# Gated cross-attention with a mixture of experts: values of four heads in quarters of the matmul array, scores in row halves, K and V without zero padding

## The chip, the cores and the metric

The kernel runs on one core of one Trainium2 chip, in float32. The metric is the device time in microseconds (us) of one execution; lower is better. Engines are named as in the profile: PE (TensorE, matmuls) and PEld (its weight loads), DVE (VectorE), ACT (ScalarE), POOL (GpSimd), SP (SyncE, here an issuer of transfers). Matmuls write to PSUM, from where DVE or ACT read.

## The reference

Four sequences of 1024 tokens with 256 features attend to 64 context rows each with 16 heads of 64; the result is multiplied by the query, projected, gated and added. A mixture of 8 experts (two of them per token) follows. Cut to what matters:

```python
# x (4, 1024, 256), ctx_1024 (4, 64, 256), 16 heads of 64
qh = einsum('bld,hdk->hblk', layernorm(x), w_qs)
kh = einsum('bld,hdk->hblk', ctx, w_ks)
vh = einsum('bld,hdk->hblk', ctx, w_vs)
attn = softmax(einsum('hblk,hbmk->hblm', qh, kh), axis=-1)
out = einsum('hblm,hbmk->hblk', attn, vh) * qh
x = x + tanh(g_xattn) * (out.reshape_heads() @ w_proj.T + b_proj)
# experts: 8, F = 1024, top 2 by gate logits, softmax over the two
h = silu(einsum('td,edf->tef', layernorm(x), w1))
x = x + tanh(g_ffn) * (einsum('tef,efd->ted', h, w2) combined by the two weights)
```

## The kernel before

**Tiling.** The 4096 tokens go in 8 groups g of 512 (two groups to a sequence, so sequence b = g // 2), a group in 4 tiles t of 128. The 16 heads go in 8 pairs p; a pair's two heads of 64 fill the 128 partitions. `NP` is 8, `DK` and `M` (head size, context rows) are both 64, `P` is 128.

**K and V.** One block `kv[b]` for each of the four sequences (L168) holds both, for each pair as a 128 x 128 block-diagonal matrix: head j has rows and columns of half j, and the other two quarters stay zero from a memset on POOL (L170). `keys` (L284) computes K of two pairs into one PSUM bank and copies it out in eight 64 x 128 pieces (L302; on DVE for the first two pairs, on ACT for the rest). `values` (L306) copies V with four 64 x 256 pieces on ACT for each bank (L323).

**Queries, scores, softmax.** `queries` (L337) makes qT, the queries of a group transposed (128 partitions of a pair, 512 tokens), in two matmuls for a pair (L341), and ACT copies them out of PSUM. `probabilities` (L352) makes the scores of a tile with 8 matmuls, one for a pair, with qT of the tile as weights and the pair's 128 x 128 K block as the streamed operand (L355). DVE takes the maximum (L364) and subtracts it (L366), ACT takes the exponential (L369), DVE sums (L371) and inverts, POOL multiplies (L374). `transpose_probabilities` (L379) transposes a pair at a time on PE (L384), and ACT copies to aT (L385).

**Values.** `attend` (L390) makes for each pair one matmul, V's block as weights and aT of the group's 512 tokens as the streamed operand (L393), into a PSUM bank of its own, and DVE multiplies the result with qT in place (L394). `project` (L396) follows with L402 and adds to the residual stream.

**Order.** The loop at L996 runs over groups and tiles: scores of this tile, transposes of the tile before it, queries of the next group (L1009), then `finish` (L944) for the group before: at t = 1 all of `attend`, at t = 2 and 3 `project`. The tile framework turns the written order into one instruction list for each engine with its own planning, so neighbouring pieces can be interleaved. Calls marked `keep_in_program_order` stay where they are written. From group 6 on pieces of the experts' work (`run_slots`) are woven in. POOL's list entries and token gathers are issued behind the newest softmax multiply (`behind_softmax`, L750).

**Buffers.** PSUM has two pools: `ps2`, two tiles of two banks each, takes the scores; `ps1`, four single banks, takes everything else (`bank`, L100), among it queries, transposes, values and projections. In SBUF blocks of one "share" take turns in a number of equal buffers: "weight" has seven (wq, wp, the four kv, and the expert weights as they come).

Of the kernel before, what the change touches and what calls it, by code (L numbers as in the profile page):

```python
# [8 lines left out]
F32 = mybir.dt.float32  # L9
I32 = mybir.dt.int32  # L10
AF = mybir.ActivationFunctionType
ALU = mybir.AluOpType
# [3 lines left out]
P = 128  # L16
# [5 lines left out]
def kernel(  # L22
# [13 lines left out]
    w2: bass.AP,  # L36
    out: bass.AP,
):

# [16 lines left out]
    nc = tc.nc  # L58

    B, L, D = x.shape  # L60
    M = context.shape[1]
    H, _, DK = w_qs.shape
    E, _, F = w1.shape
# [4 lines left out]
    GB = L // G  # L68
    NP = H // 2
# [20 lines left out]
    rows = ctx.enter_context(tc.tile_pool(name="rows", bufs=2))  # L90
# [3 lines left out]
    ps2 = ctx.enter_context(tc.tile_pool(name="ps2", bufs=2, space=PSUM))  # L94
    ps1 = ctx.enter_context(tc.tile_pool(name="ps1", bufs=4, space=PSUM))

    def block(shape, name, share):
        return blocks.tile(shape, F32, tag=share, bufs=shares[share], name=name)

    def bank(name, spare=False):  # L100

        if spare:
            return ps2.tile([P, 2, 512], F32, tag="ps2", name=name)[:, 0]
        return ps1.tile([P, 512], F32, tag="ps1", name=name)
# [60 lines left out]

    kv = [block([P, 2, NP, P], f"kv{b}", "weight") for b in range(B)]  # L168
    for t in kv:
        nc.gpsimd.memset(t, 0.0)  # L170

    ident = const.tile([P, P], F32, tag="ident", name="ident")
    make_identity(nc, ident)
# [110 lines left out]
    def keys(ctxT):  # L284
        for p0 in range(0, NP, 2):
            pk = bank(f"pk_{p0}").rearrange("p (i n) -> p i n", i=2)
            for i in range(2):
                for c in range(NC):
                    nc.tensor.matmul(
                        pk[:, i, :],  # L290
                        wk[:, c, (p0 + i) * P : (p0 + i + 1) * P],
                        ctxT[:, c, :],
                        start=(c == 0),
                        stop=(c == NC - 1),
                    )
            pkv = pk.rearrange("p i (b m) -> p b i m", m=M)
            for j in range(2):
                rows = slice(j * DK, (j + 1) * DK)
                copy = nc.scalar.copy if p0 else nc.vector.tensor_copy
                for b in range(B):  # L300
                    tc.keep_in_program_order(
                        copy(kv[b][rows, 0, p0 : p0 + 2, j * M : (j + 1) * M], pkv[rows, b])  # L302
                    )
            yield

    def values(ctxT):  # L306

        n = 512 // P
        for b0 in range(0, B, 2):
            for p0 in range(0, NP, n):  # L310
                pv = bank(f"pv_{b0}_{p0}")
                for c in range(NC):
                    nc.tensor.matmul(
                        pv,
                        ctxT[:, c, b0 * M : (b0 + 2) * M],
                        wv[:, c, p0 * P : (p0 + n) * P],
                        start=(c == 0),
                        stop=(c == NC - 1),
                    )
                pvv = pv.rearrange("p (i j k) -> p i j k", j=2, k=DK)  # L320
                for i in range(2):
                    for j in range(2):
                        nc.scalar.copy(  # L323
                            kv[b0 + i][j * M : (j + 1) * M, 1, p0 : p0 + n, j * DK : (j + 1) * DK],
                            pvv[i * M : (i + 1) * M, :, j, :],
                        )
                yield

# [5 lines left out]
    def of_pair(t, p):  # L334
        return t[p // (NP // 2)][:, p % (NP // 2), :]
# [14 lines left out]
    newest = []  # L350

    def probabilities(g, t, qT):  # L352
        sc = ps2.tile([P, NP, 2 * M], F32, tag="ps2", name=f"sc_{g}_{t}")
        for p in range(NP):
            nc.tensor.matmul(  # L355
                sc[:, p, :],
                of_pair(qT, p)[:, t * P : (t + 1) * P],
                kv[g // GB][:, 0, p, :],
                start=True,
                stop=True,  # L360
            )
        scv = sc.rearrange("p i (j m) -> p (i j) m", m=M)
        mx = small.tile([P, H], F32, tag="mx", name=f"mx_{g}_{t}")
        nc.vector.tensor_reduce(mx, scv, AX.X, ALU.max)  # L364
        pr = soft.tile([P, H, M], F32, tag="pr", name=f"pr_{g}_{t}")
        nc.vector.tensor_tensor(  # L366
            pr, scv, mx.unsqueeze(2).to_broadcast([P, H, M]), ALU.subtract
        )
        nc.scalar.activation(pr, pr, AF.Exp)  # L369
        sm = small.tile([P, H], F32, tag="sm", name=f"sm_{g}_{t}")  # L370
        nc.vector.tensor_reduce(sm, pr, AX.X, ALU.add)  # L371
        nc.vector.reciprocal(sm, sm)  # L372
        newest[:] = [
            nc.gpsimd.tensor_tensor(pr, pr, sm.unsqueeze(2).to_broadcast([P, H, M]), ALU.mult).ins  # L374
        ]
        return pr

    def transpose_probabilities(g, t, pr, aT):
        prv = pr.rearrange("p (i j) m -> p i (j m)", j=2)  # L379
        n = 512 // P  # L380
        for p0 in range(0, NP, n):
            pt = bank(f"pa_{g}_{t}_{p0}")
            for i in range(n):
                nc.tensor.transpose(pt[:, i * P : (i + 1) * P], prv[:, p0 + i, :], ident)  # L384
            nc.scalar.copy(  # L385
                aT[p0 // n][:, :, t * P : (t + 1) * P], pt.rearrange("p (i q) -> p i q", i=n)
            )

    def attend(g, pairs, qT, aT):

        for p in pairs:
            po = bank(f"po_{g}_{p}")
            nc.tensor.matmul(po, kv[g // GB][:, 1, p, :], of_pair(aT, p), start=True, stop=True)  # L393
            nc.vector.tensor_tensor(of_pair(qT, p), po, of_pair(qT, p), ALU.mult)  # L394

    def project(g, qT, t0):  # L396

        pp = bank(f"pp_{g}_{t0}").rearrange("p (t d) -> p t d", d=D)
        for i in range(2):
            t = t0 + i  # L400
            for p in range(NP):
                nc.tensor.matmul(  # L402
                    pp[:, i, :],
                    of_pair(qT, p)[:, t * P : (t + 1) * P],
                    wp[:, p, :],
                    start=(p == 0),
                    stop=(p == NP - 1),
                )
        nc.vector.scalar_tensor_tensor(
            xg[g][:, t0 : t0 + 2, :], pp, tg[:, 0:1], xg[g][:, t0 : t0 + 2, :], ALU.mult, ALU.add  # L410
        )
# [265 lines left out]
    half = len(tiles) // 2  # L677
# [264 lines left out]
    held = {}  # L942

    def finish(g, step):  # L944

        qT, aT = held[g]
        if step == 1:
            attend(g, range(NP), qT, aT)
        elif step >= 2:
            project(g, qT, (step - 2) * 2)  # L950

# [44 lines left out]
    for g in range(NG + 1):  # L996
        attention_ends = g == NG
        if g < NG:
            qT, aT = q_next, halves(f"aT_{g}")
            held[g] = (qT, aT)  # L1000
        if g + 1 < NG:
            q_next = halves(f"qT_{g + 1}", "hidden" if g % 3 == 1 else "group")
        for t in range(T):
            if g < NG:
                pr = probabilities(g, t, qT)
            if last:
                transpose_probabilities(*last)
            if g + 1 < NG:
                queries(g + 1, q_next, parts[g > 0][t])  # L1009
            if 0 <= g - 1 < NG:  # L1010
                finish(g - 1, t)
            last = (g, t, pr, aT) if g < NG else None

            if g >= GB + 1:
                b = (g - GB - 1) // GB
                after(b * GB + GB - 1, (g - GB - 1) % GB * T + t)
            if g == 0 and t == 1:
                tc.keep_in_program_order(nc.scalar.activation(tg, tg, AF.Tanh))
                tc.keep_in_program_order(
                    nc.gpsimd.tensor_scalar(bias, bias, tg[:, 0:1], None, ALU.mult)  # L1020
                )
                for h in range(2):
                    add_bias(h)
            if g + 2 < NG:
                if t == 0 and (g + 2) % GB == 0:
                    stats = ln_stats(list(range(g + 2, g + 2 + GB)), f"a{g + 2}")
                elif t == 2:
                    ln_norm(g + 2, stats, "a")
                    add_bias(g + 2)
            if g == 0:  # L1030
                next(pending_values)
            for _ in range(pieces[g][t] if g in pieces else 0):
                next(slots)
# [5 lines left out]
    for _ in slots:  # L1039
# [3 lines left out]
    _, used = nc.values_load_multi_w_load_instructions(  # L1043
        in_use[0:1, 0:1], min_val=0, max_val=NB, bass_reorder=False
    )
# [38 lines left out]
```

## Time and profile before

| | |
|---|---|
| Runs shown | 945.53, 956.56, 959.87 us; median 956.56 |
| Profiled execution | 945.0 us, of which the span is 943.3 |
| Mean granted PE clock | 0.985 |
| L355, scores on PE | 512 instructions, mean 276 ns |
| L393, values on PE | 128 instructions, mean 593 ns |
| L341, queries on PE | 256 instructions, mean 596 ns |
| L402, projection on PE | 512 instructions, mean 379 ns |
| L384, transposes of probabilities on PE | 256 instructions, mean 278 ns |
| L394, multiplies on DVE | 64 instructions, median 680 ns |

All durations come from one profiled execution. The durations of matmuls overlap, since the next one starts while the last one still passes through the array, so their sum is not the time that they take; the distance from one start to the next is. Weight loads run beside the matmul before them. Busy time of other engines costs nothing as long as PE doesn't wait for them.

### The profile page before, as it was taken

The numbers are of one execution on the slowest core, as the hardware profiler recorded it, in microseconds if no ns is written. First come the engines' busy times: TensorE is split into PE (matmuls) and PEld (weight loads), VectorE is DVE, ScalarE is ACT, GpSimd is POOL, SyncE is SP. The second block draws the span as 40 slices with busy tenths as digits, with TensorE's granted clock in tenths as the row PEclk, the third lists the DMA queues.
The fourth block names the chain that finished last, engine by engine and source line by source line (L and its number), as shares of the span: only waits on it lengthen the run. The fifth ranks groups of instructions, "written<-read, shape, count | busy, mean of one in ns | idle before, by whom it ended". The sixth has DMA issues, their size and how long they took to land. (4 is left out here: it accounts for less than half of the span.)

```text
span 943.3 us, 11358 instructions
## 1 busy us (share of the span) xinstructions
PE 904.0 (96%) x4176; PEld 703.8 (75%) x4176; DVE 327.3 (35%) x733; ACT 254.7 (27%) x390; POOL 409.8 (43%) x395
## 2 busy tenths in 40 slices
PE   6989999999999996899998999999999999999995
PEld 4555858586768766587897887777777888888884
DVE  7364485647755876444138000000000000000010
ACT  3464242433342323342123121122121121121110
POOL 3051212113532254325636656755544554555343
PEclk9999999999999999899998999999999999999998
DMA  9500000100010002724773465745444455657110
GB/s 211 175 1 0 1 23 1 45 23 24 1 45 23 23 1 88 247 68 118 183 236 108 117 224 191 256 133 165 168 168 149 142 162 196 230 165 269 59 45 30
DMA packets 87789, 106.50 MB, mean 113 GB/s; under 512 B 29348, under 2 KB 73770, under 8 KB 87728
## 3 DMA queue, kind: packets, MB, share of 16 engines
q1 hardware_dynamic: 62784, 70.50, 24.4%
q0 software_dynamic: 11840, 25.25, 8.5%
q10 hardware_dynamic: 13104, 9.96, 3.6%
q8 instruction: 35, 0.57, 0.3%
q14 instruction: 26, 0.21, 0.1%
HBM read 89.60 MB, written 17.65 MB: 114 GB/s over the span
## 5 line engine op out<-in xcount | busy, mean ns | idle before, releaser
L809 PE MATMUL ph<-xT,w 128*128 128x256 f32 (+1 forms) x960 | 242.6, 410 | 0.7 <-ACT xT L782 0.7
L865 PE MATMUL py<-w,hT 128*128 128x256 f32 x1088 | 242.6, 382 | 0.0
L865 PEld LDWEIGHTS py<-w,hT 128*128 128x128 f32 x1088 | 206.4, 192 | 27.6
L809 PEld LDWEIGHTS ph<-xT,w 128*128 128x128 f32 x960 | 182.7, 191 | 52.1 <-ACT xT L782 1.1
L817 ACT ACTIVATE hT<-ph 128x1024 f32<-128x1024 f32 (+2 forms) x80 | 71.6, 896 | 390.2 <-PE ph L809 383.7
L848 DVE TENSOR_SCALAR x<-py,ids 128x256 f32<-128x256 f32 x68 | 32.9, 483 | 403.9 <-PE py L865 370.0
L374 POOL TENSOR_TENSOR pr<-pr,sm 128x1024 f32<-128x1024 f32 x32 | 61.4, 1919 | 228.8 <-DVE sm L372 218.3
L341 PE MATMUL pq<-nT_a,wq 128*128 128x512 f32 x256 | 115.9, 596 | 0.6 <-ACT nT_a L260 0.6
L402 PE MATMUL pp<-wp,qT 128*128 128x256 f32 x512 | 113.1, 379 | 0.0
L402 PEld LDWEIGHTS pp<-wp,qT 128*128 128x128 f32 x512 | 97.1, 190 | 18.2 <-issue 5.5
L831 POOL DMA_INDIRECT x<-out_dram,ids x68 | 69.9, 1028 | 88.4 <-DMA out_dram<-x,ids 62.0
L758 POOL DMA_INDIRECT x<-normed,ids x68 | 68.2, 1003 | 45.5 <-DMA ids<-lists 26.4
L850 POOL TENSOR_TENSOR x<-x,x 128x256 f32<-128x256 f32 x68 | 49.3, 725 | 82.6 <-DVE x L848 78.6
L341 PEld LDWEIGHTS pq<-nT_a,wq 128*128 128x128 f32 x256 | 46.6, 192 | 47.7 <-issue 45.4
L508 POOL DMA_INDIRECT lists<-entry,to_row x64 | 62.4, 975 | 42.9 <-DVE entry L498 19.5
L851 POOL DMA_INDIRECT out_dram<-x,ids x68 | 69.7, 1024 | 19.2 <-POOL x L850 17.7
L355 PEld LDWEIGHTS sc<-kv,qT 128*128 128x128 f32 x512 | 62.0, 192 | 7.6 <-issue 6.2
L355 PE MATMUL sc<-kv,qT 128*128 128x128 f32 x512 | 64.4, 276 | 0.7 <-DVE pr L366 0.6
L385 ACT COPY aT<-pa 128x512 f32<-128x512 f32 x64 | 34.5, 589 | 96.0 <-PE pa L384 86.5
L393 PE MATMUL po<-aT,kv 128*128 128x512 f32 x128 | 56.5, 593 | 0.1
L364 DVE TENSOR_REDUCE mx<-sc 128x16 f32<-128x1024 f32 x32 | 38.9, 1219 | 37.3 <-PE sc L355 37.1
L371 DVE TENSOR_REDUCE sm<-pr 128x16 f32<-128x1024 f32 x32 | 38.8, 1217 | 21.9 <-ACT pr L369 21.9
(180 smaller groups left out, 652.2 us busy)
## 6 DMA issues: line engine op xcount, KB each, us to landing
w<-in_L_ffn_w_dram SPq DMA_DIRECT2D x60, 1024.0 KB, 7.6
out_dram<-x ACTq DMA_DIRECT2D x8, 512.0 KB, 3.7
normed<-keep_b ACTq DMA_DIRECT2D x8, 512.0 KB, 2.9
x<-in_x_dram SPq DMA_DIRECT2D x7, 512.0 KB, 7.5
x<-normed,ids POOLq DMA_INDIRECT x68, 5.9
x<-out_dram,ids POOLq DMA_INDIRECT x68, 4.9
out_dram<-x,ids POOLq DMA_INDIRECT x68, 2.5
wv<-in_L_xattn_w_vs_dram SPq DMA_DIRECT2D x2, 512.0 KB, 7.1
```

The costliest lines, as they stand in the source:

```text
L341: nc.tensor.matmul(pq, wq[:, c, p * P : (p + 1) * P], nT[g][:, c, :], start=(c == 0), stop=(c == NC - 1),)
L355: nc.tensor.matmul(sc[:, p, :], of_pair(qT, p)[:, t * P : (t + 1) * P], kv[g // GB][:, 0, p, :], start=True, stop=True,)
L374: nc.gpsimd.tensor_tensor(pr, pr, sm.unsqueeze(2).to_broadcast([P, H, M]), ALU.mult).ins
L393: nc.tensor.matmul(po, kv[g // GB][:, 1, p, :], of_pair(aT, p), start=True, stop=True)
L402: nc.tensor.matmul(pp[:, i, :], of_pair(qT, p)[:, t * P : (t + 1) * P], wp[:, p, :], start=(p == 0), stop=(p == NP - 1),)
L508: nc.gpsimd.indirect_dma_start(out=lists, out_offset=bass.IndirectOffsetOnAxis(ap=to_row[:, k, i : i + 1], axis=0), in_=entry[:, k, i, :], ...
L758: gather = nc.gpsimd.indirect_dma_start(out=place, out_offset=None, in_=normed[: tokens_of(s)], in_offset=bass.IndirectOffsetOnAxis(ap=ids ...
L809: nc.tensor.matmul(ph[:, i, :], a[:, c, f * P : (f + 1) * P], xT[:, c, :], start=(c == 0), stop=(c == NC - 1),)
L817: nc.scalar.activation(hT[f0 // per_tile][:, f1 : f1 + step, :], ph, AF.Silu)
L831: gather = nc.gpsimd.indirect_dma_start(out=acc[t], out_offset=None, in_=outf[:n], in_offset=bass.IndirectOffsetOnAxis(ap=ids[:, t, 0:1], ...
L851: scatter = nc.gpsimd.indirect_dma_start(out=outf[:n], out_offset=bass.IndirectOffsetOnAxis(ap=ids[:, t, 0:1], axis=0), in_=acc[t], in_off ...
L865: nc.tensor.matmul(py[t], hT[f // per_tile][:, f % per_tile, t * P : (t + 1) * P], b[:, f, :], start=(f == 0), stop=(f == NF - 1),)
```

## The change

K and V lose their padding. One tile `kT` holds K of all sequences, a pair's two heads on the two halves of the partitions; one tile `vs` holds V with the context rows of one head on partitions 0 to 63 and those of another on 64 to 127.

- The memsets go. K of two pairs is copied with one instruction for a bank, by turns on DVE and ACT.
- Scores: for each pair two matmuls in place of one, each with 64 rows (one head's half of the partitions) of qT as weights and 64 columns of K streamed. The two heads of a pair write to different banks of the score tile, which so holds the first heads of all pairs and then the second heads.
- Transposes then pair head r of pair 2q with head r of pair 2q + 1.
- Values: for two pairs (four heads) four matmuls with 64 rows and 64 columns of weights, each in a quarter of the array: rows by j (which of the two pairs), columns by r (which head of the pair). They write to two banks, each half by half. DVE's multiplies stay as they are.
- `attend` now runs in two halves: the first four pairs at t = 1 ahead of the next group's queries, the other four where it was.

```diff
-    kv = [block([P, 2, NP, P], f"kv{b}", "weight") for b in range(B)]
-    for t in kv:
-        nc.gpsimd.memset(t, 0.0)
+    kT = block([P, NP, B, M], "kT", "weight")
+    vs = block([P, B, NP, DK], "vs", "weight")
...
-            pkv = pk.rearrange("p i (b m) -> p b i m", m=M)
-            for j in range(2):
-                rows = slice(j * DK, (j + 1) * DK)
-                copy = nc.scalar.copy if p0 else nc.vector.tensor_copy
-                for b in range(B):
-                    tc.keep_in_program_order(
-                        copy(kv[b][rows, 0, p0 : p0 + 2, j * M : (j + 1) * M], pkv[rows, b])
-                    )
+            copy = nc.vector.tensor_copy if p0 % 4 == 0 else nc.scalar.copy
+
+            tc.keep_in_program_order(
+                copy(kT[:, p0 : p0 + 2].rearrange("p i b m -> p i (b m)"), pk)
+            )
...
-                pvv = pv.rearrange("p (i j k) -> p i j k", j=2, k=DK)
+                pvv = pv.rearrange("p (q j r k) -> p q j r k", j=2, r=2, k=DK)
+                q0 = p0 // 2
                 for i in range(2):
+                    to = vs[:, b0 + i].rearrange("p (r q) k -> p q r k", r=2)
                     for j in range(2):
                         nc.scalar.copy(
-                            kv[b0 + i][j * M : (j + 1) * M, 1, p0 : p0 + n, j * DK : (j + 1) * DK],
-                            pvv[i * M : (i + 1) * M, :, j, :],
+                            to[j * M : (j + 1) * M, q0 : q0 + n // 2],
+                            pvv[i * M : (i + 1) * M, :, j],
                         )
...
-        sc = ps2.tile([P, NP, 2 * M], F32, tag="ps2", name=f"sc_{g}_{t}")
+        sc = ps2.tile([P, 2, NP, M], F32, tag="ps2", name=f"sc_{g}_{t}")
         for p in range(NP):
-            nc.tensor.matmul(
-                sc[:, p, :],
-                of_pair(qT, p)[:, t * P : (t + 1) * P],
-                kv[g // GB][:, 0, p, :],
-                start=True,
-                stop=True,
-            )
-        scv = sc.rearrange("p i (j m) -> p (i j) m", m=M)
+            for r in range(2):
+                of_head = slice(r * DK, (r + 1) * DK)
+                nc.tensor.matmul(
+                    sc[:, r, p, :],
+                    of_pair(qT, p)[of_head, t * P : (t + 1) * P],
+                    kT[of_head, p, g // GB, :],
+                    start=True,
+                    stop=True,
+                )
+        scv = sc.rearrange("p r i m -> p (r i) m")
...
-        for p in pairs:
-            po = bank(f"po_{g}_{p}")
-            nc.tensor.matmul(po, kv[g // GB][:, 1, p, :], of_pair(aT, p), start=True, stop=True)
-            nc.vector.tensor_tensor(of_pair(qT, p), po, of_pair(qT, p), ALU.mult)
+        for q in range(pairs[0] // 2, pairs[-1] // 2 + 1):
+            po = [bank(f"po_{g}_{2 * q + j}") for j in range(2)]
+            for r in range(2):
+                for j in range(2):
+                    half = slice(j * M, (j + 1) * M)
+                    i = r * (NP // 2) + q
+                    nc.tensor.matmul(
+                        po[j][r * DK : (r + 1) * DK],
+                        vs[half, g // GB, i, :],
+                        of_pair(aT, i)[half],
+                        start=True,
+                        stop=True,
+                    )
+            for j in range(2):
+                own = of_pair(qT, 2 * q + j)
+                nc.vector.tensor_tensor(own, po[j], own, ALU.mult)
...
-            attend(g, range(NP), qT, aT)
+            attend(g, range(NP // 2, NP), qT, aT)
...
+            if g and t == 1:
+                attend(g - 1, range(NP // 2), *held[g - 1])
             if g + 1 < NG:
                 queries(g + 1, q_next, parts[g > 0][t])
```

## The prediction

> **What bounds the kernel now.** I read the busy times first, then the table by stage, then who waits for whom in the attention stage, then the order of the matmuls in time.
>
> The page's first part gives busy us, share and count of each engine; below it is the table by stage (stage bounds, length, then busy us of PE, weight loads, DVE, ACT, POOL, granted clock, DMA share, GB/s):
>
> ```profile
> PE 904.0 (96%) x4176; PEld 703.8 (75%) x4176; DVE 327.3 (35%) x733; ACT 254.7 (27%) x390; POOL 409.8 (43%) x395
> ```
>
> ```profile
> 20.00:370.00 350.00, 344.45 (x1650) 243.45 (x1650) 218.62 (x434) 134.10 (x220) 104.83 (x69) 1.00 0.11 30
> 370.00:382.00 12.00, 1.38 (x4) 0.69 (x4) 5.48 (x8) 0.59 (x2) 6.02 (x5) 0.70 0.83 273
> 382.00:480.00 98.00, 96.84 (x457) 79.55 (x458) 35.30 (x87) 28.38 (x39) 45.51 (x45) 0.98 0.52 145
> 480.00:885.00 405.00, 402.09 (x1803) 330.09 (x1802) 50.44 (x159) 77.67 (x103) 221.56 (x235) 0.99 0.55 178
> ```
>
> Attention fills PE from 20 to 370 us (344.45 of 350), the experts fill it from 382 to 885. DVE is at 218.62 of 350 there: not the bound. Between them lies a hole of about 10 us, in which PE waits for the first gathered tokens. The waits of PE from 60 to 360 us are one line long:
>
> ```profile
> PE pa L384 <- POOL pr L374: 0.6, 1, 0.6
> ```
>
> So the price of an edit is what it does to the time PE needs to pass its instructions. Durations do not show that, as matmuls overlap; the distance from start to start does. The timeline of PE (start, us to the end of the piece, instruction, count):
>
> ```profile
> 129.50 1.95 PE L355 MATMUL sc<-kv,qT 128*128 128x128 f32 x16
> 131.29 1.04 PE L384 MATMUL pa<-ident,pr 128*128 128x128 f32 x8
> 132.16 1.88 PE L341 MATMUL pq<-nT_a,wq 128*128 128x512 f32 x4
> 133.88 7.03 PE L393 MATMUL po<-aT,kv 128*128 128x512 f32 x16
> 140.75 1.95 PE L355 MATMUL sc<-kv,qT 128*128 128x128 f32 x16
> ...
> 395.85 1.62 PE L423 MATMUL pl<-gw,nT_b 128*128 128x8 f32 x14
> ```
>
> One tile of scores takes 131.29 - 129.50 = 1.79 us for 16 instructions: 112 ns each. One group's values take 140.75 - 133.88 = 6.87 us for 16: 429 ns each. The program writes 8 matmuls in each case; the trace has 16, so each f32 matmul is two adjacent instructions, each with its own weight load. Over the run that is 512 x 0.112 = 57.3 us of scores and 128 x 0.429 = 54.9 us of values. The last line is the clue for weight loads: 14 logits matmuls stream only 8 columns but still take (1.62 - 0.25)/13 = 105 ns or a little more each (their mean duration 0.25 us). A load of 128 columns therefore passes no faster than about 105 to 112 ns, and the scores stand at that limit already.
>
> [...]
>
> **The change, part by part.** The profiled execution took 945.0 us: span 943.3 and 1.7 around it. The runs shown have a median of 956.56 and go from 945.53 to 959.87, so the profiled one lies at their lower edge. I sum against 945.0.
>
> *Values.* Eight full matmuls of a group become 16 quarter matmuls (64 rows x 64 columns), still 512 columns streamed and two instructions each: 32 instructions. If four quarters run side by side, a group takes 32/4 x 429 ns = 3.43 us instead of 6.87. Eight groups: -27.4 us. [...]
>
> *Scores.* Eight full matmuls with 128 columns streamed become 16 with 64 rows and 64 columns streamed. Streaming halves, but the weights are still 128 columns of qT, and there are 32 loads in a tile instead of 16. If the two row halves load side by side it is 16 load times, 1.79 us as before: 0. If loads pass one at a time it is 32 x 112 = 3.58 us, +1.79 us in each of 32 tiles, +57.3 us. A gain is excluded, because the load pitch binds already. I take 0 and keep +57.3.
>
> *Mode switches.* New: full, half and quarter modes alternate. Two switches for each of 32 score tiles, and two for each of 16 half attends: 64 + 32 = 96, if nothing is interleaved. The trace has none. Lower bound 0[...]. Upper: a matmul's tail, duration less pitch (593 - 429 = 164 ns), plus an exposed load (190 ns): 0.354 us, 34 us in all. I take one exposed load at its pitch, 0.112: +10.8 us.
>
> *Attend in two halves, with pairs of banks.* The multiplies of DVE stay 64 x 0.68 us. Before, eight of them (5.4 us) lay under 6.87 us of PE. Now the first half attend puts four outputs into the four single banks in 0.86 us, right behind a score tile. DVE is then still in that tile's maximum and subtraction (1.22 each, 2.44 from the end of the scores), so the first bank is free at 2.44 + 0.68 = 3.12, while PE wants it for the queries at 0.87 (transposes) + 0.86 = 1.73. Behind that wait are the queries, the second half attend, and through ACT's qT copies the next group. Up to 1.4 us for each of 8 groups, 11 us; 0 if the compiled order has the queries first. I take 6.
>
> *K and V without padding.* Four memsets (7.04 us) leave POOL: 0, since they ended at 9.84 us and the first K copy began at 12.31, released by PE. Thirty-two K copies (8 on DVE, 0.285; 24 on ACT, 0.263) become four of 512 elements, about 0.6 to 0.7 by the ACT and DVE copies of that size at L260. DVE begins the first statistics at 14.15 right after its eight copies; one wide copy ends 1.1 us earlier, but the transposes also wait for the last key matmul at 17.8, so about 0.5 of the 1.1 arrives: -0.5 us. The 16 V copies keep number and size. Four blocks of the "weight" share become two; they free nothing for the expert weights at 371 us, since kv0 to kv2 were released by then: before, wp and kv3 are held, after, wp and vs, five free either way: 0. No DMA is added or moved; the queues of SP and POOL keep their order, their list entries following the softmax as before.
>
> Sum: 945.0 - 27.4 + 0 + 10.8 + 6 - 0.5 = 933.9 us. Savings before about 357 us pass the hole at 370, because the list entries and gathers that end it follow the softmax, which follows PE. Since two of three runs lie 1.2 and 1.5% above the profiled one, I lean up by 2: 936.
>
> **The rivals.**
>
> *Case 1*, all quarters and halves truly side by side: the sum above; its ends are 945.0 - 27.9 = 917 (switches and bank waits free) and 917 + 34 + 11 = 962.
>
> *Case 2*, the two instructions of one f32 matmul block each other. They are adjacent, on one tile, and start in order: the second waits for the first's stream, and the next tile waits behind it. Then only the second half of one overlaps with the first half of the next: one 429 ns step for each of 16 quarter matmuls, 6.87 us, no gain. With switches, and no bank wait as PE is slow again: 945.0 + 10.8 - 0.5 = 955. For it: the adjacency in the trace. [...]
>
> *Case 3*, the other side: weight loads of the two row halves pass one at a time. Place: L355's loads. 945.0 - 27.4 + 57.3 + 10.8 - 0.5 = 985; it decides as soon as more than half of the doubled loads are not overlapped (28 us). For it: scores stand at the load pitch now, and the number of 128-column loads doubles. [...]
>
> *Case 4*, the change does not do what it says: tiles take turns altogether, +54.9 on values and +57.3 on scores: about 1068.
>
> **Numbers.** Case 1: 0.58; case 2: 0.14; case 3: 0.24; case 4: 0.04. A measurement here cannot tell about 2% from no change, 19 us. Case 1 is faster by that only if switches and waits together stay under 9 us: 0.38 faster, 0.20 within. Case 2: 0.10 within, 0.04 slower (dear switches). Cases 3 and 4 slower. Together 0.38, 0.30, 0.32. Case 1 alone: 917 to 962. The range: 915 at the bottom, below which nothing is worked out, to 992, which takes in case 3 at its price and leaves out its dear half and case 4, some 0.16.
>
> **What would show it.** Values: PE from the first to the last po instruction of a group, 3.4 us (case 1) or 6.9 (case 2). Scores: 32 instructions of a tile in 1.8 us or 3.6. Switches: a gap of 0.1 to 0.35 us between the last tiled and the first full matmul. Bank waits: PE's query matmuls or loads waiting on DVE's L394 successor. I would be wrong if scores fell clearly below 1.79 us a tile (loads cheaper with 64 rows), or if the hole at 370 grew by what attention gained.

## The result and the profile after

The changed kernel is slower: a median of 968.31 us over 20 runs (958.36 to 974.74) beside 955.11 for the kernel before, a ratio of 1.0136 with a 95% interval of 1.0107 to 1.0164. That is under the 2% named in the prediction, but the interval lies wholly above 1. The profiled execution took 959.5 us, with a span of 957.7. The runs of both kernels scatter more here than later, when the kernel before had medians of about 946, but the lowest run of each gives the same ratio (958.36 / 945.52 = 1.0136), and every ratio below is against the runs of before made beside it.

The first part of the page of the changed kernel (busy us, share, count), and of the groups by shape the two that were edited:

```profile
PE 910.3 (95%) x4816; PEld 700.0 (73%) x4816; DVE 319.1 (33%) x727; ACT 253.0 (26%) x368; POOL 404.1 (42%) x391
```

```profile
L358 PE MATMUL sc<-kT,qT 64*128 64x64 f32 x1024 | 72.6, 287 | 0.9 <-issue 0.8
L402 PE MATMUL po<-aT,vs 64*64 64x512 f32 x256 | 37.7, 611 | 1.3 <-issue 1.3
```

Both edits do on PE what was intended: 1024 half and 256 quarter instructions. Their timeline in the stretch that the prediction showed:

```profile
129.22 2.00 PE L358 MATMUL sc<-kT,qT 64*128 64x64 f32 x32
131.15 1.09 PE L387 MATMUL pa<-ident,pr 128*128 128x128 f32 x8
132.17 1.95 PE L402 MATMUL po<-aT,vs 64*64 64x512 f32 x16
134.47 1.98 PE L341 MATMUL pq<-nT_a,wq 128*128 128x512 f32 x4 [0.35 <-DVE qT L411]
136.39 2.09 PE L402 MATMUL po<-aT,vs 64*64 64x512 f32 x16
138.41 2.00 PE L358 MATMUL sc<-kT,qT 64*128 64x64 f32 x32
140.34 1.09 PE L387 MATMUL pa<-ident,pr 128*128 128x128 f32 x8
```

Half an attend has 16 instructions in 1.95 us. They start in fours, 7 ns apart within a four, and the fours start 0.48, 0.43 and 0.43 us apart (from 132.17 us); full instructions that stream 512 columns, that is, pass them through the loaded weights, start 0.43 us apart as well. So four run at a time. A score tile takes 131.15 - 129.22 = 1.93 us with its 32 loads, against 1.79 before. The weight loads (PEld) show why: the thirty-two start in pairs, 7 ns apart, and pass in 1.86 us, two in the time in which one of full height passed before (0.11 us); eight of the quarters pass in 0.21, and a single one lasts 0.13. So the loads of different tiles overlap (a bracket is the idle time before the group).

```profile
129.22 1.86 PEld L358 LDWEIGHTS sc<-kT,qT 64*128 64x128 f32 x32 [0.76 <-issue]
132.17 0.21 PEld L402 LDWEIGHTS po<-aT,vs 64*64 64x64 f32 x8 [0.17 <-issue]
```

From one score tile to the next the stretch shown lasts 138.41 - 129.22 = 9.19 us, against 11.25 before. Little of that is left over a whole group of four tiles: 45.55 us, from the start of a score tile at 83.67 to the same tile of the next group at 129.22, against 45.98 before (83.52 to 129.50). So there is a small gain here; the loss is elsewhere, and the table by stage has it in one column, the granted clock (after the busy times of PE, loads, DVE, ACT and POOL). Before, then after:

```profile
70.00:180.00 110.00, 110.00 (x511) 76.51 (x510) 62.91 (x105) 41.19 (x65) 21.84 (x11) 1.00 0.05 15
180.00:330.00 150.00, 149.35 (x754) 109.62 (x753) 100.13 (x225) 51.70 (x82) 47.94 (x33) 1.00 0.08 22
```

```profile
70.00:180.00 110.00, 108.94 (x715) 73.05 (x714) 63.41 (x106) 42.27 (x66) 21.83 (x11) 1.00 0.05 15
180.00:330.00 150.00, 146.91 (x919) 106.60 (x919) 94.01 (x207) 47.37 (x75) 44.34 (x30) 0.94 0.08 22
```

From 180 to 330 us PE is busy for 146.91 of 150 us, yet its clock fell to 0.94. The clock records of both traces give full or half clock (1.0 or 0.5) and nothing between, and in each trace every record but the last lasts a whole number of times 3.413 us: in the attention stage of the changed kernel four stretches at half, from about 190, 207, 292 and 313 us, of 3.4, 3.4, 6.8 and 3.4 us, where the kernel before has none. Around the hole it stays at half for 23.9 us instead of 10.2. The first of them closely, in stretches of 3.4 us, and the instructions in it:

```profile
186.60:190.00 3.40, 3.40 (x38) 3.24 (x38) 0.59 (x4) 0.00 (x0) 0.00 (x0) 1.00 0.00 0
190.00:193.40 3.40, 3.40 (x11) 2.36 (x12) 2.43 (x2) 2.00 (x3) 0.00 (x0) 0.50 0.47 159
```

```profile
186.59 0.66 PE L358 MATMUL sc<-kT,qT 64*128 64x64 f32 x8
187.18 1.73 PE L440 MATMUL pl<-gw,nT_b 128*128 128x8 f32 x14
188.84 1.10 PE L358 MATMUL sc<-kT,qT 64*128 64x64 f32 x14
189.88 1.89 PE L387 MATMUL pa<-ident,pr 128*128 128x128 f32 x8
```

The table calls PE busy for all 3.40 us of 186.6 to 190.0, and then its clock is halved. At the pitch of 512 columns in 429 ns a column takes 0.84 ns. The 22 half matmuls run in pairs: 11 x 64 x 0.84 = 0.59 us of streaming; the 14 logits add 14 x 8 x 0.84 = 0.09, and the transpose that begins there 0.1. By this estimate PE streamed for about 0.8 of those 3.4 us, while PEld was busy for 3.24 of them. After it eight transposes take 1.89 us instead of 1.09.

### The profile page after: what moved, and what is told of

It reads as the page before. It is cut to its first block, busy times and chain, and to the rows that moved or that the text cites. A ratio compares the mean times of both kernels' runs of the same rounds, so it can differ in the third digit from the quotient of the medians.

```text
span 957.7 us, 12598 instructions
## 1 busy us (share of the span) xinstructions
PE 910.3 (95%) x4816; PEld 700.0 (73%) x4816; DVE 319.1 (33%) x727; ACT 253.0 (26%) x368; POOL 404.1 (42%) x391
## 5 line engine op out<-in xcount | busy, mean ns | idle before, releaser
L341 PE MATMUL pq<-nT_a,wq 128*128 128x512 f32 x256 | 119.7, 611 | 5.0 <-DVE qT L411 4.2
L358 PEld LDWEIGHTS sc<-kT,qT 64*128 64x128 f32 x1024 | 66.4, 197 | 17.6 <-issue 17.3
L358 PE MATMUL sc<-kT,qT 64*128 64x64 f32 x1024 | 72.6, 287 | 0.9 <-issue 0.8
L348 ACT COPY qT<-pq 128x512 f32<-128x512 f32 x64 | 36.6, 582 | 42.6 <-PE pq L341 42.6
```

Of the source, the lines that this page charges most:

```text
L341: nc.tensor.matmul(pq, wq[:, c, p * P : (p + 1) * P], nT[g][:, c, :], start=(c == 0), stop=(c == NC - 1),)
L358: nc.tensor.matmul(sc[:, r, p, :], of_pair(qT, p)[of_head, t * P : (t + 1) * P], kT[of_head, p, g // GB, :], start=True, stop=True,)
```

## The experiments

**The two halves of the change, and three rivals.** The first theory was that the scores in row halves bring the half clock, because they halve the streaming under unchanged loads. Rivals: the quarters bring it; the tiled mode itself does; or mode switches and bank waits eat the gain and the clock is by the way.

The first kernel has the values' part alone, with K padded again in blocks `kb`:

```diff
...
-                    sc[:, r, p, :],
-                    of_pair(qT, p)[of_head, t * P : (t + 1) * P],
-                    kT[of_head, p, g // GB, :],
...
+                sc[:, p // 2, :, p % 2, :],
+                of_pair(qT, p)[:, t * P : (t + 1) * P],
+                kb[g // GB // 2][:, g // GB % 2, p, :],
...
```

> Values in quarters and the attend in two halves as in the change; scores as before: full 128-row matmuls against zero-padded K (the pair's two outputs are written two heads apart so that the transposes keep the change's pairing). Clock theory (it is the scores in row halves, streaming 64 columns under loads of 128, that let the granted clock fall to half): no half-clock window between 75 and 360 us, mean clock 0.985 or better, values 3.4 to 4.5 us of PE a group, and 0.975 to 0.985 of the time before. Rival, values in quarters let the clock fall: half-clock windows stay between 180 and 360 us, mean clock 0.975 or less, ratio 0.99 or more. Rival, switches and bank waits alone eat the gain: clock 0.985 and ratio 0.99 to 1.00.

Measured: ratio 0.9904 (0.9889 to 0.9919). The table by stage and the waits of PE from 60 to 365 us:

```profile
180.00:330.00 150.00, 145.47 (x807) 105.18 (x804) 101.80 (x238) 51.69 (x82) 49.67 (x35) 1.00 0.08 22
```

```profile
PE pq L349 <- DVE qT L417: 4.2, 6, 1.3
PE pa L393 <- POOL pr L383: 1.0, 1, 1.0
PE po L408 <- DVE qT L417: 0.9, 2, 0.7
```

The clock stays at 1.00: the quarters are acquitted. The gain was smaller than I expected from the clock theory and lies in the band of the last alternative, that switches and bank waits eat it. A group's values take 5.0 us (six groups, from the starts of PE's instructions), not 3.4 to 4.5; the waits for the multiplies, 5.1 us in all, are a part of that, as the bank waits of the prediction had it.

The second has the scores' part alone; padded V and whole attend as before, and DVE's subtraction puts the heads back in pairs:

```diff
...
-            pr, scv, mx.unsqueeze(2).to_broadcast([P, H, M]), ALU.subtract
+            pr.rearrange("p (i r) m -> p r i m", r=2),
+            sc,
+            mx.rearrange("p (r i) -> p r i", r=2).unsqueeze(3).to_broadcast([P, 2, NP, M]),
+            ALU.subtract,
...
```

> Scores in row halves with compact K; values as before in full matmuls with padded V, attend in one piece (DVE's subtraction puts the heads back in pairs). Clock theory: half-clock windows between 180 and 360 us as in the change, mean clock 0.975 or less, scores about 0.3 to 0.4 us a tile dearer with their switches (10 to 13 us) plus about 10 us of half clock: ratio 1.015 to 1.03. Rival, the quarters let the clock fall: mean clock 0.985, ratio 1.005 to 1.015. Rival, scores in halves cost nothing: ratio 1.00.

Measured: ratio 1.0172 (1.0154 to 1.0190), mean clock 0.974, and from 180 to 330 us a clock of 0.95, all as the clock theory had it:

```profile
180.00:330.00 150.00, 149.51 (x874) 108.39 (x871) 92.03 (x185) 47.79 (x75) 44.36 (x30) 0.95 0.06 19
```

The loss sits in the scores.

The third keeps the halves but lets each stream 128 columns, so that loads, switches and tiling stay and only the streaming changes:

```diff
+                first = (p * B + g // GB) * M
+                wide = min(2, NP - p) * M
...
-                    sc[:, r, p, :],
+                    sc[:, r].rearrange("p i m -> p (i m)")[:, p * M : p * M + wide],
...
-                    kT[of_head, p, g // GB, :],
+                    kT.rearrange("p i b m -> p (i b m)")[of_head, first : first + wide],
```

> The changed kernel, but each score matmul streams 128 columns of K instead of 64 (the second 64 are the next columns in memory; the next pair overwrites them, and the last pair streams 64): same loads, same row halves, same number of instructions and switches, only the streaming doubles, beneath loads of the same length. Clock theory: a score tile takes no longer than in the change (about 1.9 us) and the half-clock windows between 180 and 360 us go: mean clock about 0.985, ratio 1.000 to 1.006. Rival, it is the tiled mode or its gaps that count as idle: windows stay, ratio 1.013 or more. Rival, the streaming of the two halves doesn't fit beneath the loads: a tile takes 2.5 us or more, ratio above 1.02.

Measured: ratio 1.0030 (1.0004 to 1.0055). A tile of 32 still takes 138.72 - 136.78 = 1.94 us, though each instruction streams twice as much:

```profile
136.78 2.00 PE L360 MATMUL sc<-kT,qT 64*128 64x128 f32 x32
138.72 1.09 PE L389 MATMUL pa<-ident,pr 128*128 128x128 f32 x8
```

The stretches at half clock that lay where logits and scores meet went; two others, of 3.4 us each, came at about 233 and 336 us, each after a window in which PE had waited for a bank (its queries wait 6.2 us for the multiplies in all, 2.5 the longest). More work for PE, and less time (1.0030 against 1.0136): no theory of switches or waits alone gives that.

The fourth puts the whole attend back in one place (`attend(g, range(NP), ...)` in `finish`).

> The changed kernel with all of the attend in one piece at its old place. If bank waits behind the early half attend are what eats the gain: the queries' waits for DVE (4.2 us in all) go and the ratio falls to 1.008 or less. Clock theory: eight outputs in four banks keep PE to the multiplies of DVE, 5.4 us a group against 3.4, so waits grow by about 1 us a group and half-clock windows stay: ratio 1.013 to 1.025.

Measured: ratio 1.0110 (1.0091 to 1.0130), a little under the change and under the band I gave. The waits of PE change their place, from the queries (4.2 us) to the values, also 4.2 us from 60 to 365 us, and the clock stays low (0.95 from 190 to 350 us, as in the change). The split brings nothing to the change, and costs nothing that this run can show.

**Tiling mode or streaming.** The fifth kernel is the one before, with each score matmul cut in two of 64 columns on all 128 rows. Nothing in it is tiled:

```diff
-            nc.tensor.matmul(
-                sc[:, p, :],
-                of_pair(qT, p)[:, t * P : (t + 1) * P],
-                kv[g // GB][:, 0, p, :],
+            for j in range(2):
+                nc.tensor.matmul(
+                    sc[:, p, j * M : (j + 1) * M],
+                    of_pair(qT, p)[:, t * P : (t + 1) * P],
+                    kv[g // GB][:, 0, p, j * M : (j + 1) * M],
...
```

> The kernel before with each score matmul cut in two that stream 64 columns each, on all 128 rows (the padded K, one half of its columns each): no tiling mode anywhere, twice the loads, one after the other. If the share of streaming under the loads is what the clock follows: a tile takes 32 x 112 ns = 3.6 us at full clock, in which PE streams about half of the time, and half-clock windows appear all through the attention stage (mean clock 0.95 or less), ratio 1.075 to 1.13. If the tiling mode is what counts as idle: mean clock 0.985 as before and only the loads' 57 us, ratio 1.055 to 1.065.

Measured: ratio 1.0507 (1.0487 to 1.0526), which misses both bands. A tile takes 103.38 - 99.86 = 3.52 us, so full-height loads do pass one after the other, 0.11 us each:

```profile
99.86 3.68 PE L356 MATMUL sc<-kv,qT 128*128 128x64 f32 x32
103.38 1.04 PE L385 MATMUL pa<-ident,pr 128*128 128x128 f32 x8
```

But the clock is neither low throughout nor as before:

```profile
70.00:180.00 110.00, 110.00 (x575) 81.53 (x573) 55.75 (x91) 33.05 (x53) 21.95 (x12) 1.00 0.02 6
180.00:330.00 150.00, 150.00 (x788) 113.44 (x787) 83.61 (x172) 47.33 (x72) 39.87 (x28) 0.95 0.09 25
```

It falls without any tiling, from 1.00 in the stage without gate logits to 0.95 in the one that has them. Scores alone, which by estimate stream half of the time (64 x 0.84 = 54 ns of each 110), don't bring it; scores and logits together do. That refined the theory to a share: the part of a window of 3.41 us in which PE streams. I summed it for each window from starts and shapes of the matmuls in all fourteen traces, at 0.84 ns a column, the windows laid on the grid that the clock records show. Between 75 and 360 us there are 1126 that began at full clock. Of the 32 that were followed by half clock, 31 have a share of 0.41 or less; of the 1094 that were not, none is below 0.40. The changed kernel's four are 0.27, 0.36, 0.41 and 0.39; the lowest of the kernel before is 0.47. Windows of the experts' part, from 380 us on, which were not used to find the bound, fit it too: 15 of 17 that were followed by half clock lie at 0.41 or less, and 3 of 2179 others.

One window up to 360 us does not fit (0.62), in the fourth kernel, from 346.6 to 350.0:

```profile
346.86 1.07 PE L402 MATMUL po<-aT,vs 64*64 64x512 f32 x4 [0.96 <-DVE qT L411]
347.87 0.44 PE L358 MATMUL sc<-kT,qT 64*128 64x64 f32 x4
348.80 3.28 PE L402 MATMUL po<-aT,vs 64*64 64x512 f32 x12 [0.50 <-DVE qT L411]
```

PE streams for much of it, but in quarters that waited for banks: four of them took 347.87 - 346.86 = 1.01 us up to the scores behind them, where sixteen took 138.41 - 136.39 = 2.02 in the change, so the four did not all run at once. If each matmul is counted by the part of the array that it fills, a quarter as 0.25 and a half as 0.5, this window has a share of 0.32, and all 32 lie at 0.38 or less; but then four of the 1094 others do as well. Whether the clock follows the time of streaming or the part of the array in use stays open; for scores and logits both counts say much the same.

PE's busy time doesn't tell the windows apart: in the one from 186.6 us PE has no gap (3.40 of 3.40 us busy), and the clock behind it is 0.50. The share of streaming does (0.27 in that window).

The test of the share leaves all tiled instructions alone and lets the logits stream their 8 columns sixteen times over:

```diff
...
-                    gw[:, c, :],
+                    gw[:, c].unsqueeze(1).to_broadcast([P, 16, E]),
...
```

> The changed kernel, tiling, order and scores untouched; only the gate logits stream their 8 columns sixteen times over (128 columns, one result of the sixteen used), which their 128-column loads of about 105 ns cover. Refined clock theory (PE's clock is halved for the next 3.4 us after a window of 3.4 us in which PE streams less than about 0.42 of the time, whatever the tiling mode; in the change that happens where logits and row-half scores meet): the half-clock windows between 180 and 330 us go, mean clock 0.980 or more, 7 to 9 us less than the change, ratio 1.003 to 1.008. Rival, the tiled instructions themselves count as idle: windows stay, ratio 1.012 or more.

Measured: ratio 0.9970 (0.9958 to 0.9982), better than the band. Stage table and timeline:

```profile
180.00:330.00 150.00, 147.16 (x966) 105.39 (x965) 96.93 (x219) 49.81 (x80) 46.21 (x31) 1.00 0.08 22
```

```profile
187.05 1.83 PE L440 MATMUL pl<-gw,nT_b 128*128 128x128 f32 x14
188.81 1.32 PE L358 MATMUL sc<-kT,qT 64*128 64x64 f32 x18
190.06 1.09 PE L387 MATMUL pa<-ident,pr 128*128 128x128 f32 x8
```

Fourteen logits take 1.76 us instead of 1.66, and the transposes behind them are back at 1.09. Its control is the same edit in the kernel before:

> The same widening of the logits in the kernel before, where no window between 75 and 360 us is below that share: ratio 1.000 to 1.003, mean clock 0.985. If the widening brings time by itself, 0.995 or less, and the run before this one says less than it seems.

Measured: 0.9974 (0.9966 to 0.9982), slightly better than the band: a stretch of 6.8 us at half clock near 500 us, where logits run among the experts, is gone. So of the change's way from 1.0136 to 0.9970, 0.0026 is there in the kernel before too, and some 0.014, or 13 us, is what the low clock of the scores in halves cost, with what followed from it. About 7 of the 13 stand in the clock records (half of 53.0 - 34.5 us at half clock, less half of 31.3 - 27.2 in the control); the rest arose behind the hole, among the experts' first work, and stays open. Between the two kernels with wide logits nothing is left (943.58 and 943.59 us): the change as a whole is worth nothing even without the low clock from 180 to 330 us.

**Where the values' gain went.** PE's waits for the multiplies led to a placement behind the queries, first half at tile 0, second at tile 1, in the values-alone kernel and in the change:

```diff
-        if step == 1:
+        if step == 0:
+            attend(g, range(NP // 2), qT, aT)
+        elif step == 1:
             attend(g, range(NP // 2, NP), qT, aT)
...
-            if g and t == 1:
-                attend(g - 1, range(NP // 2), *held[g - 1])
```

> Values in quarters, scores full as in the first experiment, but the first half of the attend stands behind the queries of the first tile and the second half behind those of the second, so that DVE is past its softmax steps and each half finds four banks being freed. If bank waits on DVE keep the quarters from their gain: PE's waits for the multiplies (5.6 us at 60 to 365 us) go to 1 us or less, values take 3.6 to 4 us a group, no new half-clock window, ratio 0.980 to 0.987. If the waits only move to the maximum of the next scores or to the hole: ratio stays 0.988 to 0.992.

> The changed kernel with the two halves of the attend placed as in the run before this one; scores in row halves with 64 columns streamed. Bank waits go here too, but half-clock windows in the attention stage stay (mean clock 0.975 or less): ratio 1.002 to 1.010, that is 5 to 10 us better than the change and still not faster than before. If bank waits were the main loss of the change, 0.995 or less.

> The changed kernel with the spread attend and with scores streaming 128 columns: both losses taken away, only the switches around score tiles are left of the halves. Mean clock 0.983 or better, ratio 0.988 to 0.997; above the values-alone version with the same attend by the price of 64 switches, 6 to 12 us.

All three missed: 0.9935 (0.9920 to 0.9950), 1.0114 (1.0095 to 1.0132) and 1.0139 (1.0115 to 1.0162). In the first the waits for the multiplies went, but the first line of PE's waits over the whole span, and the timeline, show a new one:

```profile
PE pa L393 <- POOL pr L383: 14.1, 6, 4.2
```

```profile
133.01 1.04 PE L393 MATMUL pa<-ident,pr 128*128 128x128 f32 x8
133.88 1.88 PE L349 MATMUL pq<-nT_a,wq 128*128 128x512 f32 x4
135.70 1.95 PE L408 MATMUL po<-aT,vs 64*64 64x512 f32 x16
137.57 3.84 PE L364 MATMUL sc<-kb,qT 128*128 128x128 f32 x32
145.59 1.97 PE L393 MATMUL pa<-ident,pr 128*128 128x128 f32 x8 [4.17 <-POOL pr L383]
```

With its attend cut to a half, tile 1 has too little PE work to cover a softmax: maximum, subtraction, exponential, sum and POOL's multiply are 1.22 + 1.22 + 1.06 + 1.22 + 1.92 = 6.6 us before any hand-over. The transposes wait for POOL, and after 4.17 us without a matmul they run at half clock (eight take 1.97 us, and 1.04 at full clock). The whole attend at that tile had been that cover. In the change the same waits came, 13.5 us in all, and 14.3 with wide scores (the last of the three), where they undid what the wide scores had given.

The eleventh kernel is the sixth with its tiles balanced, three query pairs each in the first two:

```diff
-    parts = [range(0, 2), range(2, 4), range(4, 6), range(6, 8)], [range(0, 5), [5], [6], [7]]
+    parts = [range(0, 2), range(2, 4), range(4, 6), range(6, 8)], [range(0, 3), range(3, 6), [6], [7]]
```

> Values in quarters, scores full, the attend's halves behind the queries of tiles 0 and 1 as in the sixth experiment, and two of the five query pairs of tile 0 moved to tile 1, so that tile 1 lasts longer than its softmax chain (about 7 us from scores to POOL's multiply). If the softmax chain is what came late in the sixth: the transposes' waits for POOL fall from 14 us to 4 or less, the two windows near 140 and 243 us go, ratio 0.976 to 0.985. Else 0.990 to 0.994.

Measured: ratio 0.9789 (0.9775 to 0.9803), median 926.22 us beside 946.24, with the twelfth the fastest here, faster than the kernel before and the changed one. The waits for POOL fell less than I had named, to 5.1 us instead of 4 or less, and no stretch at half clock is left between 75 and 360 us. The same line of its waits:

```profile
PE pa L393 <- POOL pr L383: 5.1, 3, 3.0
```

The same balance in the kernel before was not run; in the stretch that the prediction showed it waits for 0.6 us in all, so there is little that it could win.

> The kernel of the run before this one with widened logits. Full scores keep its windows above the share already: within 0.3% of that kernel. If windows near the logits still cost it something, 3 to 6 us less.

Measured: 0.9789 (0.9771 to 0.9806), as expected. Wide logits change nothing beside full scores (927.16 us and 926.22).

## Why the prediction was wrong

It forecast 936 us and a gain; the time lies inside its range, but moved the other way. That it lies inside is luck: no case has the clock in it, and the upper end was set by case 3, which did not come. Two steps of the sum failed. The larger is an assumption under the whole of it: "PE needs" was priced by pitches (the distance from one start to the next) taken at full clock, and the clock column, which stood in the very table that it quoted (1.00 in attention), was taken as given. The halved streaming of the scores was worked out and put down as 0; it cost 11.6 us of clock. The second is the size of the values' gain: 14.1 us where 20.6 were forecast for the same six groups.

I redid the sum from the starts of PE's instructions in the two profiled executions, from the first query to the last one before the hole (six of eight groups of values, 31 of 32 score tiles), at full clock with the clock apart:

| Term | Forecast, whole kernel | Measured in that stretch |
|---|---|---|
| Values | -27.4 (-20.6 for six groups) | -14.1, waits and switches behind them counted |
| Scores, loads | 0 | 0 |
| Mode switches | 96 x 0.112 = 10.8 | 9.9 for the 86 outside the values |
| Bank waits behind scores | 6 | 2.8; further ones are inside the values |
| Clock | not in the sum | 11.6: 26.5 us of work at half clock against 3.4 |
| Not in the sum: loads uncovered behind a switch, small waits | 0 | 4.5, what is left |

The stretch grew by 14.7 us, to which the last column adds by the choice of its last row; the hole was 0.8 us shorter. Without the clock 3.1 us of loss remain, where the sum had 11.1 of gain.

- *Values, right in mechanism.* Four quarters run at once (16 in 1.95 us), so case 2, in which the two instructions of one f32 matmul block each other, is wrong. The gain was mis-sized: waits for aT, for banks and the switches back leave two thirds of it.
- *Scores, right in price.* Loads of the two row halves overlap (1.93 us a tile; the 0.14 above 1.79 is the switch behind it), so case 3 fell too. The fifth experiment shows what it would have cost: 3.52 us a tile.
- *Switches, right.* Where a full instruction of 128 columns and a half meet, in either order, one start lies 0.20 us behind the other. Beyond the usual pitch (0.11 among the full ones, 0.06 on average among the halves) a change into tiled instructions so adds 0.09 us and one out of row halves 0.14, 0.115 on average: inside the bounds of 0 and 0.354, and near the 0.112 taken. All three were estimates, as no instruction of the trace before is tiled.
- *Bank waits.* As named: PE's queries wait 4.2 us for DVE, in six of eight groups; 1.4 of it stand right behind the values.
- *K, V and their blocks at nothing.* The first queries start half a microsecond earlier, as forecast.
- *What would make it wrong.* I had named cheaper loads and a longer hole. The hole did not grow. That PE might be given a slower clock was not on the list.

The slower side was priced for the wrong reason: case 3 put it on loads, and the largest part of what came is the clock.

## What to carry to other kernels

On an engine that is always busy, ask of an edit not only what time its instructions pass in, but how much of that time is streaming: cutting streaming beneath loads that stay gained nothing here (1.93 us a score tile against 1.79), and beside the logits, where PEld is as full (3.24 of 3.40 us), it cost clock (0.94 from 180 to 330 us against 1.00). When a saved stretch was the cover for another engine's chain, spread the remaining work before counting the gain. Try the parts of a change apart: here one part was worth 1.0% as it stood and 2.1% once the tiles were balanced, and the other cost 1.7% by itself.

## What the runs showed of the hardware

- In the traces of both kernels half clock came in stretches of 3.4 us or a multiple of it (up to 23.9), but for the last, which ends with the trace. Of the 32 windows of 3.4 us in the fourteen traces that it followed, from full clock and between 75 and 360 us, 31 had PE streaming for 0.41 of the time or less, and of the 1094 others 1 had. PE can read as busy throughout such a window (3.40 of 3.40 us from 186.6 us in the changed kernel), and the clock fell without any tiling too (0.95 from 180 to 330 us in the fifth kernel). Counted by the part of the array in use, all 32 had 0.38 or less, and 4 of the others. What sets the clock is not shown beyond these counts.
- Widening an instruction beneath its weight load cost 0.01 us a score tile (1.94 us with 128 columns in the third kernel, 1.93 with 64) and 0.10 us for 14 logits (1.76 us with 128 columns, 1.66 with 8); with wide logits the change went from 1.0136 to 0.9970.
- Weight loads of two row halves, and of four quarters, overlap (32 in 1.86 us, eight in 0.21, in the changed kernel); 32 loads of full height with 64 columns streamed pass one at a time (3.52 us in the fifth kernel).
- Between full instructions of 128 columns and row halves 0.20 us pass from start to start, 0.09 more than among full ones and 0.14 more than among halves (the changed kernel).
